# Head of a graph-block kernel: the edge chain moved forward in the written order, its spreading transposes set behind a later product, and one block's one-hot rows moved from ScalarE to VectorE

## The chip, the cores and the metric

The kernel runs on one core of one Trainium2 chip. The metric is the device time of one execution in microseconds (us): the median of three runs, and beside it one profiled execution whose instructions are all recorded. The engines are TensorE (PE, with its weight loads in rows called PEld), VectorE (DVE), ScalarE (ACT), GpSimd (POOL) and SyncE (SP, which here only issues transfers).

## The reference

A graph block on 1250 nodes of 512 features, with 41250 directed edges sorted by destination. Cut to what matters:

```python
xn = layernorm(x)
h  = prelu(xn @ lin_W.T + lin_b, lin_a)
for l in range(2):
    agg = segment_sum(h[src], dst)              # sum over the edges
    h = prelu((h + agg) @ W1[l].T + b1[l], a[l]) @ W2[l].T + b2[l]
    h = relu(batchnorm(h))
x = x + h + linear_attention(xn)                # softmaxed q and k, 8 heads
x = x + merged_experts_ffn(layernorm(x))
```

## The kernel before, in words

The 1250 rows of `x` are ten tiles of up to 128 rows. The kernel turns the edge list into a dense matrix `adj` (source by destination, one added on the diagonal), so that the sum over edges becomes a matrix product. To build `adj`, the sorted edges are cut into 81 blocks of 512. For each block, a window of 24 destinations is found; two sets of one-hot rows are made, `oh_s` (128 wide, by the source's low bits) and `oh_k` (240 wide, by the source's high bits and the destination inside the window); four products on TensorE multiply them, and VectorE adds the 128x240 result to `adj` at the window.

Before any block can be made, the window's start must be known, and this is the **edge chain** of the head, in this order:

- ScalarE copies the destinations to floats (`e_d`, line 746).
- VectorE takes, for each partition, the smallest destination of a block, masks the padding, and takes the largest: three instructions (lines 748, 750 and 751), with the result in `ends`.
- TensorE transposes both halves of `ends` into two PSUM banks `pts` (line 759).
- VectorE reduces each over 128 columns to `span` (line 762).
- TensorE transposes `span` again, broadcast over 128 rows, into `lows` and `highs` (lines 771 and 772; the spreading products).
- VectorE makes `base` (774), its integer copy `base_i` (776) and, in four steps, `key` (784, 785, 788 and 789), and from the sources `s_hi` (766) and `s_lo` (794).

The edges come in by three transfers on SP's queue (lines 661, 663 and 665), which stand behind four tiles of `x` and the four parts of `lw`, and ahead of tiles 4 to 9 of `x`.

The other work of the head is the layer norm of the ten tiles and the first linear layer. Per tile `t`: `x_first(t)` is two VectorE instructions for mean and variance (586, 588) and a square root on ScalarE (590); `x_second(t)` is a reciprocal and a small product on VectorE (595, 596) and the normalising pass on ScalarE (600); `x_third(t)` is four transposes on TensorE and a copy on ScalarE (606, 607). `lin(c0, cn, f)` is eight recorded products on TensorE over `cn` nodes (576), two passes on ScalarE (612, 613, into `h_t` and `u`), and one VectorE instruction that joins them (614).

The order of all this on TensorE, VectorE and ScalarE is written out by hand: the statements stand between `head.enter_context(given(engines={E.PE, E.DVE, E.Activation}))` and `head.close()`, and each of the three engines runs its share in the order of the statements. After `head.close()` a planner, with costs and due times of its own, sets the order at compile time; what is not bound by the written order may also be placed into its gaps. `weave(us)` puts blocks between the products at a pace of 0.70 blocks per planned microsecond; blocks 0 to 2 are made inside the head, the rest behind it. A block's four products are issued once two later blocks have been made (`keep=2`); `oh_s` and `oh_k` have four buffers each.

In every third block ScalarE makes `oh_s` instead of VectorE (`source_rows`: four passes, line 817, and one over all four rows, line 818). The test is `b % 3 == 1 and b > 3`, so block 4 is the first of these, then 7, 10 and so on.

Of the kernel before, what the change touches and what calls it, by code (L numbers as in the profile page):

```python
# [9 lines left out]
F32 = mybir.dt.float32  # L10
# [4 lines left out]
ALU = mybir.AluOpType  # L15
AX = mybir.AxisListType

P = 128
N = 1250
# [12 lines left out]
J = 4  # L32
EB = P * J
NB = (EDGES + EB - 1) // EB
# [10 lines left out]
def rows(t):  # L45
    return min(P, N - t * P)
# [479 lines left out]
def usual_block(  # L526
# [23 lines left out]
    nc = tc.nc  # L550
# [11 lines left out]
    def bank(dtype=F32):  # L562
        return psum.tile([P, 512], dtype, tag="bank", name="bank")
# [10 lines left out]
    def gemm(ps, cn, lhs, rhs, k=DT):  # L574
        for c in range(k):
            nc.tensor.matmul(ps[:, :cn], lhs(c), rhs(c), start=(c == 0), stop=(c == k - 1))  # L576
# [6 lines left out]
    def spread(src, n):  # L583

        st = small.tile([P, 6], F32, name="st")
        nc.vector.bn_stats(st[:n], src)
        mv = small.tile([P, 2], F32, name="mv")
        nc.vector.bn_aggr(mv[:n], st[:n])
        rs = small.tile([P, 2], F32, name="rs")
        nc.scalar.activation(rs[:n, 0:1], mv[:n, 1:2], AF.Sqrt, bias=eps[:n])  # L590
        return mv, rs

    def inverse(mv, rs, n):

        nc.vector.reciprocal(rs[:n, 0:1], rs[:n, 0:1])
        nc.vector.scalar_tensor_tensor(rs[:n, 1:2], mv[:n, 0:1], -1.0, rs[:n, 0:1],
                                       op0=ALU.mult, op1=ALU.mult)

    def normal(dst, src, rs, n):
        nc.scalar.activation(dst, src, AF.Identity, bias=rs[:n, 1:2], scale=rs[:n, 0:1])  # L600

    def to_features(dst, t, src, n):

        pt = bank()
        for c in range(DT):
            nc.tensor.transpose(pt[:, c * P:c * P + n], src[:, c * P:(c + 1) * P], ident[0:n, 0:n])  # L606
        nc.scalar.copy(dst[:, :, t * P:t * P + n], pt.rearrange("p (c n) -> p c n", c=DT)[:, :, 0:n])  # L607

    def prelu(dst, ps, cn, bias, slope):

        u = tmp.tile([P, CHUNKS[0][1]], F32, tag="xt", bufs=4, name="u")
        nc.scalar.activation(dst, ps[:, :cn], AF.Relu, bias=v(*bias))  # L612
        nc.scalar.activation(u[:, :cn], ps[:, :cn], AF.Relu, bias=minus(*bias), scale=-1.0)  # L613
        nc.vector.scalar_tensor_tensor(dst, u[:, :cn], minus(*slope), dst, op0=ALU.mult, op1=ALU.add)  # L614
# [7 lines left out]
    early = count.enter_context(tc.tile_pool(name="early", bufs=1))  # L622
# [22 lines left out]
    edges = early.tile([P, NB, 2, J], I32, name="edges")  # L645
# [50 lines left out]
    def x_first(t):  # L696
        x_live[t] = spread(x_in[0:rows(t), t, :], rows(t))

    def x_second(t):
        n = rows(t)  # L700
        mv, rs = x_live.pop(t)
        inverse(mv, rs, n)
        normal(xn[0:n, t, :], x_in[0:n, t, :], rs, n)

    def x_third(t):
        to_features(xn_t, t, xn[0:rows(t), t, :], rows(t))
# [3 lines left out]
    def lin(c0, cn, f):  # L710
        ps = bank()
        gemm(ps, cn, lambda c: lw[:, c, f * P:(f + 1) * P], lambda c: xn_t[:, c, c0:c0 + cn])
        prelu(h_t[:, f, c0:c0 + cn], ps, cn, ("lin_b", f), ("lin_a", f))
# [22 lines left out]
    x_second(3)  # L736
    lin(0, 256, 0)
    x_third(2)
    x_first(4)
    lin(0, 256, 1)  # L740
    x_third(3)
    x_second(4)
    x_first(5)
    lin(0, 256, 2)
    e_d = early.tile([P, NB, J], F32, name="e_d")
    nc.scalar.copy(e_d, edges[:, :, 1, :])
    ends = early.tile([P, 2, NB], F32, name="ends")
    nc.vector.tensor_reduce(ends[:, 0, :], e_d, AX.X, ALU.min)
    real = early.tile([P, NB, J], F32, name="real")
    nc.vector.scalar_tensor_tensor(real, e_d, float(N), e_d, op0=ALU.is_lt, op1=ALU.mult)  # L750
    nc.vector.tensor_reduce(ends[:, 1, :], real, AX.X, ALU.max)
    x_second(5)
    lin(0, 256, 3)
    x_third(4)
    x_first(6)
    pts = [bank(), bank()]
    lin(256, 256, 0)
    for k in range(2):
        nc.tensor.transpose(pts[k][0:NB, 0:P], ends[:, k, :], ident)
    span = early.tile([NB, 2], F32, name="span")  # L760
    for k, op in ((0, ALU.min), (1, ALU.max)):
        nc.vector.tensor_reduce(span[:, k:k + 1], pts[k][0:NB, 0:P], AX.X, op)
    x_second(6)

    s_hi = early.tile([P, NB, J], I32, name="s_hi")
    nc.vector.tensor_scalar(s_hi, edges[:, :, 0, :], 7, None, op0=ALU.logical_shift_right)
    lin(256, 256, 1)
    x_third(5)
    x_first(7)
    lows, highs = bank(), bank()  # L770
    nc.tensor.transpose(lows[:, 0:NB], span[:, 0:1].to_broadcast([NB, P]), ident[0:NB, 0:NB])
    nc.tensor.transpose(highs[:, 0:NB], span[:, 1:2].to_broadcast([NB, P]), ident[0:NB, 0:NB])
    base = const.tile([P, NB], F32, name="base")
    nc.vector.tensor_scalar(base, lows[:, 0:NB], float(N - W), None, op0=ALU.min)
    base_i = early.tile([1, NB], I32, name="base_i")
# [37 lines left out]
    def source_rows(b, oh_s):  # L813

        off = hot.tile([P, J, P], F16, bufs=2, name="off")
        for j in range(J):
            nc.scalar.activation(off[:, j, :], count16[:, 0:P], AF.Abs, bias=s_lo[:, b, j:j + 1], scale=-1.0)
        nc.scalar.activation(oh_s, off, AF.Relu, bias=1.0, scale=-1.0)  # L818

    def weave(us, keep=2):  # L820

        state["due"] += us * PACE
        while state["block"] < min(NB, state["due"]):
            b = state["block"]
            state["block"] += 1
            oh_s = hot.tile([P, J, P], F16, name="oh_s")
            oh_k = hot.tile([P, J, NT * W], F16, name="oh_k")
            if b % 3 == 1 and b > 3:
                source_rows(b, oh_s)
            for j in range(J):  # L830
                if b % 3 != 1 or b <= 3:
                    nc.vector.tensor_scalar(oh_s[:, j, :], count16[:, 0:P], s_lo[:, b, j:j + 1], None,  # L832
                                            op0=ALU.is_equal)
                nc.vector.tensor_scalar(oh_k[:, j, :], count16, key[:, b, j:j + 1], None, op0=ALU.is_equal)  # L834
            held.append((b, oh_s, oh_k))
            drain(keep)

    def drain(keep):
        while len(held) > keep:
            b, oh_s, oh_k = held.pop(0)  # L840
            if b % 16 == 0:
                k = min(16, NB - b)
                _, state["at"] = nc.values_load_multi_w_load_instructions(
                    base_i[0:1, b:b + k], engines=[mybir.EngineType.DVE], min_val=0, max_val=N - W,
                    skip_runtime_bounds_check_because="both ends are taken from 0 to N - W",
                )
            ps = bank()
            for j in range(J):
                nc.tensor.matmul(ps[:, 0:NT * W], oh_s[:, j, :], oh_k[:, j, :], start=(j == 0), stop=(j == J - 1))  # L849
            at = ds(state["at"][b % 16], W)  # L850
            nc.vector.tensor_tensor(adj_r[:, :, at], adj[:, :, at],  # L851
                                    ps[:, 0:NT * W].rearrange("p (s d) -> p s d", s=NT), ALU.add)
# [3 lines left out]
    for f in range(1, DT):  # L856
        weave(1.4)
        lin(512, 384, f)
        if f < 3:
            x_third(f + 7)  # L860
    head.close()
    for f in range(DT):
        weave(2.4)
        lin(896, 354, f)
# [13 lines left out]
    def k_stage(f):  # L878
        parts = []
        k_m = small.tile([P, 4], F32, name="k_m")  # L880
        for b, (c0, cn) in enumerate(CHUNKS):
            weave(2.8)
            ps = bank()
            gemm(ps, cn, lambda c: wk[:, c, f * P:(f + 1) * P], lambda c: xn_t[:, c, c0:c0 + cn])
            nc.vector.tensor_reduce(k_m[:, b:b + 1], ps[:, :cn], AX.X, ALU.max)
            parts.append(ps)
        nc.vector.tensor_reduce(k_m[:, 3:4], k_m[:, 0:3], AX.X, ALU.max, negate=True)
        k_s = small.tile([P, 4], F32, name="k_s")
        for b, (c0, cn) in enumerate(CHUNKS):
            nc.scalar.activation(k_rows(f)[:, c0:c0 + cn], parts[b][:, :cn], AF.Exp,  # L890
                                 bias=k_m[:, 3:4], accum_out=k_s[:, b:b + 1])

        nc.vector.tensor_reduce(k_s[:, 3:4], k_s[:, 0:3], AX.X, ALU.add)
        nc.vector.tensor_scalar(k_s[:, 3:4], k_s[:, 3:4], float(N) * HD ** 0.5, None, op0=ALU.mult)
        nc.vector.reciprocal(k_z[:, f:f + 1], k_s[:, 3:4])
# [516 lines left out]
def graph_block(tc, *args):  # L1412

    unusual = usual_block(tc, *args)
    with tc.If(unusual > 0):
        general_block(tc, *args)
# [58 lines left out]
```

## Time and profile before

| | us |
|---|---|
| median of three runs | 576.74 (576.42 to 578.34) |
| profiled execution | 576.46 |
| its span, first to last instruction | 574.1 |
| TensorE busy | 546.5 (95%) |
| VectorE busy | 322.7 (56%) |
| ScalarE busy | 241.0 (42%) |
| GpSimd busy | 80.1 (14%) |
| mean granted TensorE clock | 0.981 |

Times inside the execution are counted from the first instruction. An idle stretch ahead of an instruction stands in square brackets with what ended it. TensorE is busy nearly throughout, so only the stretches in which it is not are worth reading closely; the head, the first 60 us, has most of those of the first half.

### The profile page before, as it was taken

The page shows a single profiled execution, that of the slowest core. Times are in us where ns is not written, and L with a number is a line of the kernel's source. Part 1 is how long each engine was busy: PE and PEld are TensorE (multiplying, and loading weights), DVE is VectorE, ACT ScalarE, POOL GpSimd, SP SyncE. Part 2 cuts the span into 40 slices and gives each one's busy share as a digit, 9 for nine tenths or more (in the row PEclk, how much of TensorE's full clock was granted, in tenths as well). Part 3 has the DMA queues.
Part 4 walks back from the last instruction along what each step waited for, and adds up shares of the span by engine and source line. Part 5 has one row for each costly group of instructions (what it writes and reads, how often), then busy time and mean ns, then how long its engine had stood idle before and what let it go on. Part 6 is the DMA issues. An engine that isn't in the chain of part 4 may idle for free.

```text
span 574.1 us, 6955 instructions
## 1 busy us (share of the span) xinstructions
PE 546.5 (95%) x2367; PEld 369.2 (64%) x2367; DVE 322.7 (56%) x1096; ACT 241.0 (42%) x533; POOL 80.1 (14%) x77
## 2 busy tenths in 40 slices
PE   8799999999999999999999999999999989997990
PEld 7665568799955477777854454459995557764540
DVE  4579999977889635444435433111122257707793
ACT  5676654454444112332334433112334355727342
POOL 7200000000000000000013421000000001105975
PEclk9999999999999999999999999999999999997995
DMA  9400200020030020000301002000009020402023
GB/s 287 175 1 1 74 2 1 1 74 2 1 128 20 0 74 0 1 1 1 127 21 55 18 1 73 0 0 1 2 6 365 31 74 1 146 1 75 0 76 110
DMA packets 19285, 29.10 MB, mean 51 GB/s; under 512 B 1529, under 2 KB 8185, under 8 KB 19240
## 3 DMA queue, kind: packets, MB, share of 16 engines
q1 hardware_dynamic: 18984, 28.32, 14.8%
q8 instruction: 20, 0.33, 0.3%
q10 hardware_dynamic: 256, 0.25, 0.2%
q14 instruction: 25, 0.20, 0.1%
HBM read 26.01 MB, written 2.56 MB: 50 GB/s over the span
## 4 chain that ended last, share of the span: by engine, by line
PE 88%; DVE 4%; ACT 3%; POOL 2%; issue 1%; DMA 1%; POOLq 0%; DVEq 0%; ACTq 0%
PE bank L576 28%; PE bank L981 16%; PE bank L968 12%; PE bank L917 6%; PE bank L1034 6%; PE bank L1061 6%; PE bank L849 5%; PE bank L1314 3%; PE bank L606 2%; PE bank L1363 1%; POOL m L1395 1%; POOL m L1396 1%; PE bank L902 1%; DVE bank L1301 1%; PE bank L932 1%
## 5 line engine op out<-in xcount | busy, mean ns | idle before, releaser
L981 PE MATMUL bank<-adj,y_h 128*128 128x416 f32 (+1 forms) x240 | 86.5, 361 | 1.1 <-DVE adj L851 1.1
L981 PE MATMUL bank<-adj,y_l 128*128 128x416 f32 (+1 forms) x240 | 84.4, 352 | 0.0
L834 DVE TENSOR_SCALAR oh_k<-count,e_d 128x240 f16<-128x240 f16 x324 | 82.7, 275 | 0.0
L1080 POOL TENSOR_TENSOR m<-m,ls_bc 128x512 f32<-128x512 f32 (+1 forms) x10 | 12.7, 1268 | 448.8 <-ACT m L600 448.8
L968 PE MATMUL bank<-w,h_t 128*128 128x512 f32 (+1 forms) x160 | 70.4, 592 | 0.0
L576 PE MATMUL bank<-z_t,w 128*128 128x416 f32 (+1 forms) x192 | 68.9, 513 | 0.0
L576 PEld LDWEIGHTS bank<-z_t,w 128*128 128x128 f32 x192 | 36.1, 189 | 31.8 <-issue 30.4
L832 DVE TENSOR_SCALAR oh_s<-count,s_lo 128x128 f16<-128x128 f16 x220 | 54.3, 247 | 0.0
L968 PEld LDWEIGHTS bank<-w,h_t 128*128 128x128 f32 (+1 forms) x160 | 29.4, 188 | 34.8 <-issue 34.5
L614 DVE SCALAR_TENSOR_TENSOR z_t<-u,m_sb,z_t 128x416 f32<-128x416 f32 (+1 forms) x24 | 15.7, 653 | 59.8 <-ACT u L613 59.8
L981 PEld LDWEIGHTS bank<-adj,y_h 128*128 128x128 f32 x240 | 45.1, 188 | 2.6 <-issue 2.1
L981 PEld LDWEIGHTS bank<-adj,y_l 128*128 128x128 f32 x240 | 45.2, 188 | 1.2 <-issue 0.7
L849 PE MATMUL bank<-oh_k,oh_s 128*128 128x240 f16 x324 | 41.3, 266 | 1.3 <-ACT oh_s L818 1.2
L849 PEld LDWEIGHTS <-oh_s 128*128 128x128 f16 x324 | 31.6, 98 | 15.7 <-issue 4.9
L612 ACT ACTIVATE z_t<-bank,v_sb 128x416 f32<-128x416 f32 (+1 forms) x24 | 14.6, 608 | 61.5 <-PE bank L981 61.5
L851 DVE TENSOR_TENSOR adj<-adj,bank 128x240 f32 x81 | 32.3, 399 | 13.9 <-PE bank L849 12.5
L917 PE MATMUL bank<-kk,xn 128*128 128x128 f32 (+1 forms) x320 | 38.4, 275 | 0.0
L995 DVE BATCH_NORM_STATS2 bst<-h_t 128x6 f32<-128x416 f32 (+1 forms) x24 | 14.3, 595 | 42.5 <-ACT h_t L994 42.5
L576 PE MATMUL bank<-xn_t,lw 128*128 128x256 f32 (+2 forms) x128 | 37.6, 439 | 0.3 <-ACT xn_t L607 0.3
L917 PEld LDWEIGHTS bank<-kk,xn 128*128 128x128 f32 (+1 forms) x320 | 37.0, 192 | 0.1
L1061 PE MATMUL bank<-mixer,q_t 128*128 128x512 f32 (+1 forms) x80 | 36.1, 592 | 0.0
L1034 PE MATMUL bank<-wq,xn_t 128*128 128x512 f32 (+1 forms) x80 | 36.0, 592 | 0.0
(165 smaller groups left out, 797.0 us busy)
## 6 DMA issues: line engine op xcount, KB each, us to landing
t<-in_tv_w SPq DMA_DIRECT2D x12, 512.0 KB, 7.4
w<-in_conv_w SPq DMA_DIRECT2D x4, 1024.0 KB, 5.3
x_in<-in_x SPq DMA_DIRECT2D x9, 256.0 KB, 4.7
xt<-in_x SPq DMA_DIRECT2D x9, 256.0 KB, 4.2
out<-m SPq DMA_DIRECT2D x9, 256.0 KB, 2.4
rest<-in_tv_w SPq DMA_DIRECT2D x4, 512.0 KB, 5.1
lw<-in_lin_w SPq DMA_DIRECT2D x4, 256.0 KB, 4.8
wk<-in_w_qkv SPq DMA_DIRECT2D x1, 1024.0 KB, 7.0
```

Source lines behind the costliest of these rows:

```text
L576: nc.tensor.matmul(ps[:, :cn], lhs(c), rhs(c), start=(c == 0), stop=(c == k - 1))
L614: nc.vector.scalar_tensor_tensor(dst, u[:, :cn], minus(*slope), dst, op0=ALU.mult, op1=ALU.add)
L832: nc.vector.tensor_scalar(oh_s[:, j, :], count16[:, 0:P], s_lo[:, b, j:j + 1], None, op0=ALU.is_equal)
L834: nc.vector.tensor_scalar(oh_k[:, j, :], count16, key[:, b, j:j + 1], None, op0=ALU.is_equal)
L849: nc.tensor.matmul(ps[:, 0:NT * W], oh_s[:, j, :], oh_k[:, j, :], start=(j == 0), stop=(j == J - 1))
L851: nc.vector.tensor_tensor(adj_r[:, :, at], adj[:, :, at], ps[:, 0:NT * W].rearrange("p (s d) -> p s d", s=NT), ALU.add)
L917: nc.tensor.matmul(ps[:, c * P:(c + 1) * P], xn[0:n, t, c * P:(c + 1) * P], k_nodes(f)[0:n, t, :], start=(t == 0), stop=(t == NT - 1))
L968: nc.tensor.matmul(ps[:n], h_t[:, c, t * P:t * P + n], w1[:, c, :], start=(c == 0), stop=(c == DT - 1))
L981: nc.tensor.matmul(ps[:, :cn], y[0:n, s, f * P:(f + 1) * P], adj_r[0:n, s, c0:c0 + cn], start=(s == 0 and y is ys[0]), stop=(s == NT - 1 a ...
L1034: nc.tensor.matmul(ps[:n], xn_t[:, c, t * P:t * P + n], wq[:, c, :], start=(c == 0), stop=(c == DT - 1))
L1061: nc.tensor.matmul(ps[:n], q_t[:, h, t * P:t * P + n], mixer[:, h, :], start=(h == 0), stop=(h == DT - 1))
L1314: nc.tensor.matmul(ps[:, :cn], m1[:, c, f * P:(f + 1) * P], xn2_t[:, c, c0:c0 + cn], start=(c == 0), stop=(c == DT - 1))
```

## The change

In the head, six groups of statements change their place in the written order, and one test gets another bound:

- `e_d` on ScalarE moves from behind `lin(0, 256, 2)` to behind `x_third(2)`.
- The three VectorE instructions that make `ends` move from behind `lin(0, 256, 2)` to behind `x_first(4)`, ahead of `lin(0, 256, 1)`.
- The two transposes into `pts` and the two reductions into `span` move from behind `lin(256, 256, 0)` to behind `x_second(5)`, ahead of `lin(0, 256, 3)`.
- `s_hi` moves from behind `x_second(6)` to ahead of it, before `lin(256, 256, 0)`, and `x_second(6)` now stands behind that product.
- `lows` and `highs` stay behind `lin(256, 256, 1)` but move ahead of `x_third(5)` and `x_first(7)`.
- In `weave`, the bound `b > 3` becomes `b > 6` (and `b <= 3` becomes `b <= 6`): block 4's `oh_s` is made by VectorE; ScalarE's first block is 7.

```diff
     x_third(2)
+    e_d = early.tile([P, NB, J], F32, name="e_d")
+    nc.scalar.copy(e_d, edges[:, :, 1, :])
     x_first(4)
+    ends = early.tile([P, 2, NB], F32, name="ends")
+    nc.vector.tensor_reduce(ends[:, 0, :], e_d, AX.X, ALU.min)
+    real = early.tile([P, NB, J], F32, name="real")
+    nc.vector.scalar_tensor_tensor(real, e_d, float(N), e_d, op0=ALU.is_lt, op1=ALU.mult)
+    nc.vector.tensor_reduce(ends[:, 1, :], real, AX.X, ALU.max)
     lin(0, 256, 1)
     x_third(3)
     x_second(4)
     x_first(5)
     lin(0, 256, 2)
-    e_d = early.tile([P, NB, J], F32, name="e_d")
-    nc.scalar.copy(e_d, edges[:, :, 1, :])
-    ends = early.tile([P, 2, NB], F32, name="ends")
-    nc.vector.tensor_reduce(ends[:, 0, :], e_d, AX.X, ALU.min)
-    real = early.tile([P, NB, J], F32, name="real")
-    nc.vector.scalar_tensor_tensor(real, e_d, float(N), e_d, op0=ALU.is_lt, op1=ALU.mult)
-    nc.vector.tensor_reduce(ends[:, 1, :], real, AX.X, ALU.max)
     x_second(5)
-    lin(0, 256, 3)
-    x_third(4)
-    x_first(6)
     pts = [bank(), bank()]
-    lin(256, 256, 0)
     for k in range(2):
         nc.tensor.transpose(pts[k][0:NB, 0:P], ends[:, k, :], ident)
     span = early.tile([NB, 2], F32, name="span")
     for k, op in ((0, ALU.min), (1, ALU.max)):
         nc.vector.tensor_reduce(span[:, k:k + 1], pts[k][0:NB, 0:P], AX.X, op)
-    x_second(6)
+    lin(0, 256, 3)
+    x_third(4)
+    x_first(6)
     s_hi = early.tile([P, NB, J], I32, name="s_hi")
     nc.vector.tensor_scalar(s_hi, edges[:, :, 0, :], 7, None, op0=ALU.logical_shift_right)
+    lin(256, 256, 0)
+    x_second(6)
     lin(256, 256, 1)
-    x_third(5)
-    x_first(7)
     lows, highs = bank(), bank()
     nc.tensor.transpose(lows[:, 0:NB], span[:, 0:1].to_broadcast([NB, P]), ident[0:NB, 0:NB])
     nc.tensor.transpose(highs[:, 0:NB], span[:, 1:2].to_broadcast([NB, P]), ident[0:NB, 0:NB])
+    x_third(5)
+    x_first(7)
...
-            if b % 3 == 1 and b > 3:
+            if b % 3 == 1 and b > 6:
                 source_rows(b, oh_s)
             for j in range(J):
-                if b % 3 != 1 or b <= 3:
+                if b % 3 != 1 or b <= 6:
```

## Prediction

> **What bounds the kernel now.** I read the page first, then the waits of the first 60 us, then each engine's timeline there, and last the granted clock by the microsecond. The page says that only TensorE's gaps are worth anything:
>
> ```profile
> PE 546.5 (95%) x2367; PEld 369.2 (64%) x2367; DVE 322.7 (56%) x1096; ACT 241.0 (42%) x533; POOL 80.1 (14%) x77
> ```
>
> TensorE's timeline shows three gaps of the edge chain and its blocks (start, duration, then the idle time before it):
>
> ```profile
> 19.60 0.31 PE L759 MATMUL bank<-ident,ends 128*81 128x128 f32 x1 [0.63 <-DVE rs L595]
> ...
> 24.52 0.28 PE L771 MATMUL bank<-ident,span 81*128 81x81 f32 x1 [2.44 <-DVE span L762]
> ...
> 47.65 0.28 PE L849 MATMUL bank<-oh_k,oh_s 128*128 128x240 f16 x1 [1.20 <-ACT oh_s L818]
> ```
>
> Together 4.27 us, and the change aims at all three. But TensorE's waits are not the head's chain. The chain of waits runs, up to 24 us, back and forth between VectorE and ScalarE. VectorE's timeline shows what the edge chain puts into it:
>
> ```profile
> 14.77 0.48 DVE L614 SCALAR_TENSOR_TENSOR h_t<-u,m_sb,h_t 128x256 f32<-128x256 f32 x1 [1.15 <-ACT u L613]
> ...
> 18.05 0.48 DVE L748 TENSOR_REDUCE ends<-e_d 128x81 f32<-128x324 f32 x1
> 18.45 0.48 DVE L750 SCALAR_TENSOR_TENSOR real<-e_d 128x324 f32<-128x324 f32 x1
> 18.96 0.49 DVE L751 TENSOR_REDUCE ends<-real 128x81 f32<-128x324 f32 x1
> 19.37 0.15 DVE L595 RECIPROCAL rs<-rs 128x1 f32<-128x1 f32 x1
> ...
> 24.18 0.48 DVE L762 TENSOR_REDUCE span<-bank 81x1 f32<-81x128 f32 x2
> 24.58 0.15 DVE L595 RECIPROCAL rs<-rs 128x1 f32<-128x1 f32 x1
> ```
>
> The reciprocals of tiles 5 and 6 stand behind the edge chain, and ScalarE waits for them:
>
> ```profile
> 13.71 0.29 ACT L590 ACTIVATE rs<-mv,eps 128x1 f32<-128x1 f32 x1 [0.96 <-DVE mv L588]
> ...
> 17.35 0.46 ACT L746 CAST e_d<-edges 128x324 f32<-128x324 int32 x1
> 19.75 0.81 ACT L600 ACTIVATE xn<-x_in,rs 128x512 f32<-128x512 f32 x1 [1.95 <-DVE rs L596]
> ```
>
> From 37 us VectorE makes one-hot rows, and up to 76 us it is as tight as TensorE:
>
> ```profile
> 51.70 0.59 DVE L614 SCALAR_TENSOR_TENSOR h_t<-u,m_sb,h_t 128x354 f32<-128x354 f32 x1 [0.24 <-ACT u L613]
> ...
> 54.50 0.59 DVE L614 SCALAR_TENSOR_TENSOR h_t<-u,m_sb,h_t 128x354 f32<-128x354 f32 x1 [0.62 <-ACT u L613]
> ...
> 74.85 0.66 DVE L834 TENSOR_SCALAR oh_k<-count,e_d 128x240 f16<-128x240 f16 x3
> 75.02 0.98 PE L849 MATMUL bank<-oh_k,oh_s 128*128 128x240 f16 x8
> ```
>
> Block 19's rows end at 75.51 and TensorE takes the last at 75.74: a slack of 0.23 us (0.05 at block 2, 0.20 at block 11). Afterwards it grows: block 32's rows end at 98.44, and TensorE takes them at 103.14. So a gain reaches the end only if VectorE too comes to block 19 earlier; behind that TensorE alone sets the pace.
>
> **The change, part by part.** One engine's instruction is costed by the distance to its successor's start.
>
> (a) `e_d` on ScalarE: 0.36 us, now behind tile 2's copy, which starts at 12.17 and frees the engine at about 12.66. There lies the 0.96 us wait shown at 13.71: cost nothing. If that cover failed, 0.36 us would fall on the chain. The edges must have landed. The second of their three transfers lands at 10.77, and packets under 512 bytes, which only these edges have in numbers there, fill 9.25 to 10.0. The third transfer's landing is not shown; tile 5 of x, issued behind it, lands at 12.16. A rule speaks against leaning on that: "DMA: Bandwidth & Descriptors", Queues, rings and completion order, says that transfers of one issuing engine do not complete in order. By the rows I take 11.5 and no wait; by the rule the landing is open, and each 1 us beyond 13.1 would hold the square root of tile 4 and all of ScalarE behind it by 1 us. I go by the packets.
>
> (b) The three instructions of `ends`, 18.05 to 19.37, are 1.32 us on VectorE's path. At the new place they start behind tile 4's variance, at 13.67, in the 1.15 us wait shown at 14.77, and free the engine at 14.96: 0.15 to 0.19 too late. Net -1.15 us for tile 5's reciprocal and what follows.
>
> (c) The two reductions to `span` (24.18 to 24.58, 0.40 us) now stand behind tile 5's reciprocal, about 18.55 to 18.95, where VectorE next waits for `u` of `lin(0, 256, 3)` (1.60 us at 21.32 before). Net -0.40 us for tile 6 on. `s_hi` (0.40 us) moves from one wait into another: nothing; without that wait it costs its 0.40.
>
> (d) TensorE: the transposes into `pts` take 0.24 us and wait about 0.2 for `ends`, so `lin(0, 256, 3)` starts 0.46 later, at 15.2. It ends near 17.1, and ScalarE takes it at 19.3: covered. The spreading products come behind `lin(256, 256, 1)` at 20.9, and `span` is ready at 19.0: the waits of 0.63 and 2.44 us go. `lin(256, 256, 2)` starts 3.3 us earlier. But what is late next is ScalarE, only 1.55 us earlier: tile 6's transposes need its normalised rows (24.3, a wait of 1.0), `lin(512, 384, 0)` needs tile 6's copy (27.9, a wait of 1.5), tile 9 costs another 0.6. Of 3.3 us, about 1.75 are given back; the first block and `s_lo` come 1.55 us earlier. PSUM: by this lay-out at most seven of the eight banks are held at once (lows and highs until 29), so no bank wait is added. No transfer is moved in any queue; SP and POOL issue what they did, in the same order.
>
> (e) Block 4: VectorE gets four instructions of 0.163, +0.65 us; ScalarE loses four passes of 0.29 and one of 0.66. TensorE's 1.20 us wait becomes a wait for VectorE, whose first pair of block 4 now comes at 46.33 + 0.36 + 0.1 (hand-over) = 46.8 instead of ScalarE's 47.60, and whose last pair comes 0.65 later: I keep 0.6 of the 1.20. `lin(896, 354, 1)` and `(…, 2)` then end earlier, and VectorE's idle 0.24 and 0.62 us, which waited for their `u`, close: -0.86. An idle 0.42 us at 43.65, behind five ScalarE passes of which some belonged to block 4, should close by about half: -0.2; how the planner refills ScalarE there is not shown, so 0 to -0.42.
>
> (f) The clock. Before, the clock granted fell after the 2.44 us gap:
>
> ```profile
> 26.00:27.00 1.00, 1.00 (x4) 0.75 (x3) 0.47 (x2) 0.97 (x3) 0.00 (x0) 0.59 0.00 0
> ...
> 29.00:30.00 1.00, 1.00 (x5) 0.82 (x4) 0.96 (x4) 0.66 (x2) 0.00 (x0) 0.70 0.00 0
> ```
>
> (the last number but two is the clock). Half speed for 3.3 us costs TensorE 1.6 us, yet VectorE set block 2's time, so little of it reached the end. Afterwards the gaps are 1.0 and 1.5 us. "TensorE: Matmul & The Clock Gate", HAM oscillation, warns of idle gaps over about 3.4 us: by that rule the dip before should not have come and none comes after. The row shows that 2.44 was enough, so gaps of 2.5 in total within 5 us may do it too. One such dip costs TensorE 1.6 us; laid over the gaps of (d) it delays the first block's products by 0.1 to 0.9, all before VectorE's limit at block 2. By rule or row my sum is the same; I count 0.
>
> The sum at block 19: -1.55 + 0.65 - 0.86 - 0.2 = -1.96 us. Behind it the rest moves as a whole. The profiled execution took 576.46 (0.28 under the median): 576.46 - 1.96 = 574.5 us.
>
> **The rivals.**
> 1. A part only: the waits stay in other places (a dip that outlasts the slack by 1 us, block 4 still late, nothing closed at 51.70 and 54.50). Without the 0.86 and the 0.2: -0.9, so 575.6. For it: the planner sets the order from 44 us on anew, and slack at blocks 2, 11, 15 and 19 is under 0.25.
> 2. All gaps pass through: -4.27, so 572.2. For it: TensorE is 95% busy and heads the chain from 25 us. Against: tile 6's rows and copy above.
> 3. Slower, by the clock: the gaps that replace one long one are spread over 23 to 38 us and keep the clock at half for four stretches of 3.4 us, 13.6 us in all. TensorE loses 6.8 us. It has the waits of 1.5, 0.6 and 0.2 in the head to absorb 2.3 of it, the 0.6 won at block 4, and the lead of 1.55: +2.35 us, so 578.8. It decides once the dip is longer than about 9 us, twice the sum of these covers. For it: a dip of 6.9 us stands at 521.1 in this trace, after several short gaps. Against: the dip of the head before ended after 3.3 us.
> 4. The edges are not there at 12.66: each late microsecond is lost; +1 us lands at 575.4.
>
> **How the numbers follow.** The forecast has 0.52; rival 1 (with 4) 0.24; rival 2 0.10; rival 3 0.14. A measurement of this kernel tells about 0.3% (1.7 us) from no change. The forecast's own range, 573.6 to 575.2 from the bounds in (e) and 0.4 of hand-over, lies mostly past that line (0.42 of 0.52); rival 2 is faster; rival 1 is within it; of rival 3, 0.12 is slower. So faster 0.52, same 0.36, slower 0.12. The range leaves out rival 2's and rival 3's far ends: 572.6 to 577.2.
>
> **What would show it.** No wait at lines 759 above 0.3 us and none at 771; tile 5's normalising pass near 18.6 instead of 19.75; `s_lo` near 35.1 instead of 36.69; new TensorE waits for ScalarE (lines 606 and 576) of about 2.5 us in total between 23 and 29; block 4's wait near 0.6 and from VectorE; block 19 taken near 73.6. Wrong would be: `s_lo` 3 us earlier (rival 2), a clock of 0.5 for over 9 us before 45 (rival 3), `e_d` waiting for a transfer (rival 4), or a block beyond 19 that makes TensorE wait.

## The result, and the profile after

The changed kernel takes 575.92 us (median of ten runs, 574.24 to 576.37) against 576.98 of the kernel before; the ratio is 0.9971, with a 95% interval of 0.9958 to 0.9985. The forecast was 574.5 us for a profiled execution of 576.46, a ratio of 0.9966. The measured 0.29% lies on the 0.3% line between "faster" and "the same", where the forecast had leaned to "faster".

The profiled execution of the changed kernel shows none of this at first sight: it took 576.37 us with a span of 574.4, against 574.1 before. The gain must be looked for by stage. TensorE's timeline in the head, with the transposes of `ends` at line 755 now and the first spreading product at 769:

```profile
14.91 0.57 PE L755 MATMUL bank<-ident,ends 128*81 128x128 f32 x2
...
20.95 0.23 PE L769 MATMUL bank<-ident,span 81*128 81x81 f32 x1
...
24.25 0.66 PE L606 MATMUL bank<-ident,xn 128*128 128x128 f32 x4 [0.83 <-ACT xn L600]
...
27.85 2.85 PE L576 MATMUL bank<-xn_t,lw 128*128 128x384 f32 x8 [1.22 <-ACT xn_t L607]
...
45.28 0.26 PE L849 MATMUL bank<-oh_k,oh_s 128*128 128x240 f16 x1 [0.38 <-DVE oh_k L834]
```

The waits of 0.63 and 2.44 us at the edge chain are gone. In their place TensorE waits 0.83 us for tile 6's normalised rows and 1.22 us for its copy (`lin(512, 384, 0)` at line 576 needs it); block 4's wait has fallen from 1.20 to 0.38 and is for VectorE. VectorE's timeline:

```profile
13.65 0.46 DVE L743 TENSOR_REDUCE ends<-e_d 128x81 f32<-128x324 f32 x1
...
18.19 0.15 DVE L595 RECIPROCAL rs<-rs 128x1 f32<-128x1 f32 x1
18.37 0.16 DVE L596 SCALAR_TENSOR_TENSOR rs<-mv,rs 128x1 f32<-128x1 f32 x1
18.45 0.48 DVE L758 TENSOR_REDUCE span<-bank 81x1 f32<-81x128 f32 x2
...
35.14 0.49 DVE L794 SCALAR_TENSOR_TENSOR s_lo<-s_hi,edges 128x324 f32<-128x324 int32 x1
...
42.52 0.62 DVE L614 SCALAR_TENSOR_TENSOR h_t<-u,m_sb,h_t 128x384 f32<-128x384 f32 x1 [0.42 <-ACT u L613]
```

Tile 5's reciprocal starts at 18.19 instead of 19.37, and `s_lo` at 35.14 instead of 36.69. ScalarE's timeline answers to it:

```profile
12.75 0.48 ACT L740 CAST e_d<-edges 128x324 f32<-128x324 int32 x1
13.82 0.29 ACT L590 ACTIVATE rs<-mv,eps 128x1 f32<-128x1 f32 x1 [0.60 <-DVE mv L588]
...
18.57 0.81 ACT L600 ACTIVATE xn<-x_in,rs 128x512 f32<-128x512 f32 x1 [0.94 <-DVE rs L596]
```

`e_d` fills part of the old 0.96 us wait and itself waits for nothing. The 0.24 and 0.62 us waits of VectorE near 52 and 54 us have no counterpart: from 48 to 56 us its timeline shows no wait at all. Block 19's last product is taken at 73.72 (75.74 before), and block 80's first at 199.74 (201.75 before): 2.01 us ahead, and the stretch between is carried over as a whole. These are the two products on TensorE, after and then before:

```profile
73.72 0.26 PE L849 MATMUL bank<-oh_k,oh_s 128*128 128x240 f16 x1
...
199.74 0.57 PE L849 MATMUL bank<-oh_k,oh_s 128*128 128x240 f16 x4
```

```profile
75.74 0.27 PE L849 MATMUL bank<-oh_k,oh_s 128*128 128x240 f16 x1
...
201.75 0.57 PE L849 MATMUL bank<-oh_k,oh_s 128*128 128x240 f16 x4
```

The 2.01 us are lost late in this one execution. In both kernels TensorE has a gap of 1.89 us near 466 us, where it waits for ScalarE's last pass of a batch norm (line 1008). Again after and then before:

```profile
466.01 1.07 PE L1151 MATMUL bank<-ident,h_t 128*128 128x128 f32 x5 [1.89 <-ACT h_t L1008]
466.91 5.29 PE L1061 MATMUL bank<-mixer,q_t 128*128 128x512 f32 x8
```

```profile
468.05 1.06 PE L1151 MATMUL bank<-ident,h_t 128*128 128x128 f32 x5 [1.89 <-ACT h_t L1008]
468.95 3.60 PE L1061 MATMUL bank<-mixer,q_t 128*128 128x512 f32 x8
```

By the microsecond (the last number but two is the granted clock), the changed kernel's profiled execution:

```profile
467.00:468.00 1.00, 1.00 (x3) 0.34 (x2) 0.93 (x4) 0.21 (x1) 0.00 (x0) 0.72 0.00 0
...
469.00:470.00 1.00, 1.00 (x3) 0.48 (x2) 0.96 (x3) 0.99 (x2) 0.00 (x0) 0.50 0.00 0
470.00:471.00 1.00, 1.00 (x3) 0.43 (x2) 0.96 (x4) 0.00 (x0) 0.00 (x0) 0.57 0.00 0
```

The eight products behind the gap take 5.29 us there, and 3.60 in the profiled execution of before, whose clock stays at 1.00 at this place. That is 1.69 us given back. A last 0.6 goes near 528 us, at the end of a fall of the clock of 6.83 us that both executions have, at 521.1 us before and at 522.1 after. The execution of before has its other fall at 26 to 30 us instead, in the head. So both show a mean clock of 0.981, and the two spans agree by accident.

### The profile page after: what moved, and what is told of

Its sections match the earlier page's. It is cut to its first block, busy times and chain, and to the rows that moved or that the text cites. A ratio compares the mean times of both kernels' runs of the same rounds, so it can differ in the third digit from the quotient of the medians.

```text
span 574.4 us, 6950 instructions
## 1 busy us (share of the span) xinstructions
PE 548.2 (95%) x2367; PEld 368.4 (64%) x2367; DVE 323.0 (56%) x1100; ACT 240.0 (42%) x528; POOL 80.2 (14%) x77
## 4 chain that ended last, share of the span: by engine, by line
PE 86%; DVE 3%; ACT 3%; DMA 3%; POOL 2%; SPq 1%; issue 1%; POOLq 0%; DVEq 0%; ACTq 0%
PE bank L576 25%; PE bank L981 16%; PE bank L968 12%; PE bank L1061 6%; PE bank L917 6%; PE bank L1034 6%; PE bank L849 6%; PE bank L1314 3%; DMA g2bc<-in_g2b_col 2%; PE bank L606 1%; PE bank L1363 1%; POOL m L1395 1%; DMA edges<-in_e_full 1%; POOL m L1396 1%; PE bank L902 1%
## 5 line engine op out<-in xcount | busy, mean ns | idle before, releaser
L849 PE MATMUL bank<-oh_k,oh_s 128*128 128x240 f16 x324 | 43.0, 266 | 0.6 <-DVE oh_k L834 0.4
L1061 PE MATMUL bank<-mixer,q_t 128*128 128x512 f32 (+1 forms) x80 | 37.8, 615 | 0.0
L576 PE MATMUL bank<-xn_t,wk 128*128 128x416 f32 (+1 forms) x96 | 36.2, 514 | 0.0
```

What stands on the lines that cost most here:

```text
L1061: nc.tensor.matmul(ps[:n], q_t[:, h, t * P:t * P + n], mixer[:, h, :], start=(h == 0), stop=(h == DT - 1))
```

## The experiments

Two theories stood against each other after the forecast. The first: the alternation of VectorE and ScalarE sets the head's pace, and the gain is what leaves that chain, carried on because VectorE sets the pace up to block 19. The second: TensorE's waits are the gain. Executions start with some tenths of scatter (tile 2's normalising pass starts between 9.20 and 9.73), so in this table block 80's first product is counted from that pass, and set against the 192.55 us of before.

Four recorded executions with the changed kernel's head agree in this count within 0.07 us. Two with the head of before do not: in the one whose gap at 466 us is filled it is 192.86, because there the half clock of the head came 1.0 us earlier, ScalarE waited 0.17 us for `lin(256, 256, 2)`, and `s_lo` and all behind it came 0.30 later. So a difference of up to 0.3 us from before says nothing, and the changed kernel's gain is 2.1 to 2.4 us.

| kernel | tile 2's pass | `s_lo` | wait at the spreading products | wait at block 4 | block 80's first product | counted from the pass, against before |
|---|---|---|---|---|---|---|
| before | 9.20 | 36.69 | 2.44 | 1.20 | 201.75 | 0 |
| changed | 9.31 | 35.14 | 0 | 0.38 | 199.74 | -2.12 |
| head alone | 9.21 | 34.98 | 0 | 1.20 | 200.04 | -1.72 |
| block 4 alone | 9.30 | 36.80 | 2.44 | 0.38 | 201.39 | -0.46 |
| spreading products later | 9.50 | 37.22 | 0.80 | 1.20 | 202.28 | +0.23 |
| `ends` alone | 9.73 | 35.94 | 1.85 | 1.20 | 201.01 | -1.27 |
| another order on top (`s_lo` itself moved forward) | 9.39 | 25.79 | 0 | 0 | 197.28 | -4.66 |

Counted from the pass, block 80 moves with `s_lo` in every one of these kernels but the last: `s_lo` comes 1.67 us earlier in the changed kernel, 1.72 with the head alone, 1.28 with `ends` alone, and 0.22 later with the spreading products later. Block 80 follows each to 0.01 us, and where block 4's rows are on VectorE another 0.46 is added. So what counts is when VectorE can start the rows.

**The head alone.** The changed kernel with the old bound of `source_rows`:

```diff
-            if b % 3 == 1 and b > 6:
+            if b % 3 == 1 and b > 3:
-                if b % 3 != 1 or b <= 6:
+                if b % 3 != 1 or b <= 3:
```

> The changed kernel with block 4's one-hot rows left on ScalarE. By the forecast (the head's gain is what the VectorE-ScalarE chain wins, 1.55 us, and block 4's move adds 0.4): s_lo at 35.1 to 35.2 as in the changed kernel; TensorE waits about 1.2 us at block 4 for ScalarE; block 80's first product at about 200.2 (201.75 before, 199.74 changed); time 1.5 us under before. By the rival that block 4's move is the whole gain: block 80 at 201.7 and no gain.

Median 575.35 (22 runs) against 577.19 before; ratio 0.9971 (0.9962 to 0.9981). The head carries 1.72 of the 2.12 us, and block 4's wait for ScalarE is 1.20 as before:

```profile
45.94 0.28 PE L849 MATMUL bank<-oh_k,oh_s 128*128 128x240 f16 x1 [1.20 <-ACT oh_s L818]
```

**Block 4 alone.** The kernel before with the new bound:

```diff
-            if b % 3 == 1 and b > 3:
+            if b % 3 == 1 and b > 6:
-                if b % 3 != 1 or b <= 3:
+                if b % 3 != 1 or b <= 6:
```

> The kernel before with block 4's rows on VectorE and nothing else changed. By the forecast: s_lo stays at 36.7, TensorE's wait at block 4 falls from 1.20 to about 0.5, VectorE's 0.24 and 0.62 us waits near 52 and 54 close and pay for the added 0.65, so block 80's first product comes at about 201.35 (0.4 earlier than before). By the rival that block 4's move is the gain: 199.7, 2 us earlier.

Median 577.05, ratio 0.9994 (0.9984 to 1.0004). The 0.46 us at block 80 are there, where 0.4 was expected; the time itself cannot tell them from nothing. By itself this is little more than the 0.3 by which before differs from itself; but with the head moved too the new bound is worth 0.40 (2.12 less 1.72), between heads that scatter by 0.07. The two parts add up: 1.72 and 0.46 against 2.12 together. The rival that block 4 is the gain falls.

**The spreading products later, and nothing else.** The kernel before with `lows`, `highs`, `base` and `base_i` moved behind `lin(256, 256, 2)`:

```diff
     lin(256, 256, 1)
     x_third(5)
     x_first(7)
-    lows, highs = bank(), bank()
...
     lin(256, 256, 2)
+    lows, highs = bank(), bank()
...
     x_third(6)
```

> The kernel before with only the two spreading products, and base and base_i behind them, moved behind lin(256, 256, 2): it takes TensorE's 2.44 us wait away without freeing VectorE or ScalarE of anything. By the forecast: the wait at the spreading products is gone, the same time comes back as waits for tile 6's rows and copy, s_lo stays within 0.2 of 36.69, block 80's first product within 0.3 of 201.75, time unchanged. By the rival that TensorE's waits are the gain: block 80 at about 199.4 and 2.4 us saved.

Median 577.09, ratio 1.0006 (0.9997 to 1.0015). TensorE's timeline of this kernel shows what became of the 2.44 us:

```profile
24.76 0.26 PE L772 MATMUL bank<-ident,span 81*128 81x81 f32 x1 [0.80 <-DVE span L762]
...
25.97 0.66 PE L606 MATMUL bank<-ident,xn 128*128 128x128 f32 x4 [0.76 <-ACT xn L600]
...
29.57 2.85 PE L576 MATMUL bank<-xn_t,lw 128*128 128x384 f32 x8 [1.21 <-ACT xn_t L607]
```

0.80 us of waiting is left at the spreading products (it had been expected to vanish), and 1.97 us come back as waits for tile 6. `s_lo` and block 80 come 0.5 us later than before, outside the 0.2 and 0.3 that were expected, but 0.3 of it is the later start of this execution: counted from the pass it is 0.22 and 0.23. So 1.64 us of waiting taken from TensorE, without freeing the other two engines, is worth nothing here, where the second theory wanted 2.4. This decides between the two theories.

**`ends` alone.** The kernel before with only `e_d` and the three instructions of `ends` at their new places:

```diff
     x_third(2)
+    e_d = early.tile([P, NB, J], F32, name="e_d")
...
     x_first(4)
+    ends = early.tile([P, 2, NB], F32, name="ends")
...
     lin(0, 256, 2)
-    e_d = early.tile([P, NB, J], F32, name="e_d")
...
     x_second(5)
```

> The kernel before with only e_d and the three instructions of ends moved forward to where the changed kernel has them; the transposes, the reductions to span and the spreading products stay, and so does block 4 on ScalarE. By the forecast's terms: VectorE's chain wins 1.15 us (s_lo at 35.5 instead of 36.69), while TensorE still waits 2 to 2.5 us at the spreading products; block 80's first product 1.15 earlier, at 200.6; time 1.1 us under before. By the rival that TensorE's wait is what counts: its wait stays, so no gain.

Median 576.96 against 577.22, ratio 0.9983 (0.9972 to 0.9994). TensorE still waits at the spreading products, and block 80 comes 1.27 us earlier:

```profile
23.76 0.28 PE L771 MATMUL bank<-ident,span 81*128 81x81 f32 x1 [1.85 <-DVE span L762]
```

That is term (b), forecast at 1.15. By itself this run does not tell the theories apart: the wait at the spreading products fell by 0.59 and the one of 0.63 at line 759 is gone, so TensorE too waits 1.22 less. The medians differ by only 0.26, where 1.1 was expected: half of these runs have the mean clock of 0.978, and about a third of before's. Between runs of one mean clock it is 1.05 (577.25 against 578.30 at 0.978) and 0.80 (575.44 against 576.24 at 0.984).

**The gap at 466 us filled.** The changed kernel, and the kernel before, each with 16 transposes that nobody reads:

```diff
     last_order.enter_context(given())
+    dead = bank()
+    for i in range(16):
+        nc.tensor.transpose(dead[:, 0:P], ident, ident)
```

> The changed kernel with 16 transposes of the identity that nobody reads, put into TensorE's 1.89 us gap at 464 to 466 us. Theory: the changed kernel gains 2.0 us up to block 80, and in most runs pays 1.7 of them back where the clock falls to 0.5 from 467.3 to 470.7. Then with the gap filled the clock stays 1.00 there in every run, the mean granted clock is 0.984 throughout, and the median falls by 1.5 to about 574.4. If the dip is not due to that gap: 0.981 and about 576 as without the filling, or 0.1 to 0.3 us more for the dead products.

> The kernel before with the same 16 unread transposes in the same gap, here at 466 to 468 us. If the clock's fall behind that gap comes in some of its runs (those near 578.3) and not in others (near 576.4), then with the gap filled the slower group is gone and the median comes to about 576.6; the changed kernel with the same filling (574.7) then stands 1.9 to 2.0 us under it, which is the gain of the head alone. If the two groups of times have another cause, they stay.

Changed and filled: 574.70 us (573.74 to 574.85, five runs). Before and filled: 576.51 (575.88 to 577.61), which is 0.9985 (0.9976 to 0.9995) of before unfilled. The filled pair differs by 1.81 us, expected 1.9 to 2.0; the two were measured in different sets, whose unfilled kernel before stood at 577.19 and 577.22. In the filled changed kernel no run is left near 576, where eight of the unfilled kernel's first ten were, and neither filled profile shows a fall of the clock at that place. One filled run still has a mean clock of 0.981, so the mean alone doesn't say where the clock fell. Of the filled kernel before no run lies above 577.61, where the unfilled one has 17 of 43 above 578; but a group of four runs remains at 577.25 to 577.61, with a mean clock of 0.978 or 0.979, and no trace shows where their clock fell.

**Once more, and later.** Does the change itself bring that fall of the clock, by making the gap come 2 us earlier? The changed kernel was run again, and once with 19 unread transposes ahead of the second layer's first product:

```diff
+    dead = bank()
+    for i in range(19):
+        nc.tensor.transpose(dead[:, 0:P], h_t[:, DT - 1, 0:P], ident)
     ys = y_stage(1, h_t, w1, ("C", "D"), lambda t: None)
```

> The changed kernel once more, for the share of its runs that pay for the clock's fall behind the gap at 466 us (mean clock 0.981 against 0.984): 8 of its first 10 runs did, and about a third to a half of the runs of before. If the change itself brings the fall (because that gap now comes 2 us earlier), about 8 in 10 again and a median near 576.0. If the share is one half whatever the kernel: a median near 575.3 and 3 us under the slow group of before.

> The changed kernel with 19 unread transposes of h_t (2.07 us) ahead of the second layer's first product, so that everything from there on, the gap at 466 included, comes at the same time as in the kernel before. If the fall of the clock hangs on that time, its share drops to that of before and the median is 2.07 - 0.8 above the changed kernel's, near 577.0. If it does not, the share stays and the median is 2.07 above the changed kernel's in the same call, near 578 or 577.4.

The second set of the changed kernel: 574.29 us against 577.02, ratio 0.9948 (0.9928 to 0.9967), with one of six runs near 576 instead of eight of ten. Its profiled execution has the same head (block 80 at 199.71) and a span of 572.1, because the clock stays:

```profile
467.00:468.00 1.00, 1.00 (x4) 0.46 (x3) 0.93 (x4) 0.18 (x1) 0.00 (x0) 1.00 0.00 0
...
469.00:470.00 1.00, 1.00 (x4) 0.49 (x3) 0.97 (x3) 0.96 (x2) 0.00 (x0) 1.00 0.00 0
```

Of all 16 runs of the changed kernel, nine have the lower clock (median 575.9) and seven the higher (574.2). The delayed kernel took 577.35 us, 3.06 above the changed kernel beside it, with 12 of 22 runs at the lower clock. Its median falls between the two expectations and decides nothing; 9 in 16 and 12 in 22 are about the same share, so there is no sign that the fall hangs on the gap's time. With eight of ten in one set and one of six in the next, shares of so few runs can't say more. The unread products cost 2.5 us within the group of the higher clock (576.74 against 574.24) instead of 2.07. In the trace all that stands behind them comes 2.35 us later, and the gap ends at 468.35.

**Which executions pay.** The twelve traces say more than the shares. In each, the granted clock changes only on a grid: every stretch at one clock that begins and ends inside the execution is a multiple of 3.41 us, and the grid lies differently against the program each time. In the changed kernel's first profile, 0.72 in the row of 467 and 0.57 in that of 470 put the fall at 467.4 to 470.9, and the grid interval ahead of it, 464.0 to 467.4, holds the whole gap (464.1 to 466.0). In its second profile a grid line at 464.7 cuts the gap in two, and the clock stays. Up to 500 us there are seven falls in all twelve, each behind an interval with 1.74 to 2.45 us of idle TensorE; the most idle time that no fall follows is 1.83. If the grid lies at random, the gap of 1.89 us lies within one interval in (3.41 - 1.89) / 3.41 = 45% of executions, an estimate from these numbers and near 9 in 16. No run moved the grid on purpose, and near 520 us idle time alone does not tell: falls come there behind as little as 0.5 us of it.

**Another order on top.** If the alternation of VectorE and ScalarE is the pace, more can be had from it. The changed kernel with these moves:

```diff
-    x_second(5)
     pts = [bank(), bank()]
...
     x_third(4)
+    x_second(5)
     x_first(6)
...
-    x_second(6)
     lin(256, 256, 1)
+    x_second(6)
...
+    s_lo = early.tile([P, NB, J], F32, name="s_lo")
+    nc.vector.scalar_tensor_tensor(s_lo, s_hi, -float(P), edges[:, :, 0, :], op0=ALU.mult, op1=ALU.add)
+    x_first(8)
     key = e_d
...
     x_first(9)
+    nc.vector.tensor_tensor(key, key, real, ALU.add)
+    nc.vector.scalar_tensor_tensor(key, s_hi, float(W), key, op0=ALU.mult, op1=ALU.add)
     lin(512, 384, 0)
```

> The changed kernel with a few more statements of the head in another order: x_second(5) behind x_third(4), x_second(6) behind lin(256, 256, 1), x_first(8) and s_lo ahead of key, the last two steps of key behind x_first(9). If the alternation of VectorE and ScalarE sets the head's pace (ScalarE waits for a tile's reciprocal while a finished product stands ready for it), then s_lo and key are ready 4 us earlier, block 0's first product comes 2.8 earlier than in the changed kernel (34.4 instead of 37.22), and block 80's 2.5 to 3.5 earlier (196.7); time about 573.0 with a clock of 0.981. If TensorE or the rest of VectorE's queue sets the pace instead, at most 1 us.

> The same order with the gap at about 462 us filled as well. Theory: the clock stays at 1.00 there, so the time is the filled changed kernel's 574.7 less 2.5 to 3.5, near 571.7: under both kernels. If the later order does not help: 574.7.

571.61 us (571.46 to 571.83, four runs): 0.9896 (0.9875 to 0.9917) of before, and under both kernels. ScalarE's timeline shows one part of the mechanism:

```profile
17.60 0.47 ACT L612 ACTIVATE h_t<-bank,v_sb 128x256 f32<-128x256 f32 x1
...
19.41 0.81 ACT L600 ACTIVATE xn<-x_in,rs 128x512 f32<-128x512 f32 x1 [0.50 <-DVE rs L596]
```

`lin(0, 256, 3)`'s passes start at 17.60, as soon as the product is done, instead of standing at 19.29 behind tile 5's normalising pass, which waits for VectorE. Tile 5 itself comes 0.84 later (19.41 against 18.57), but the products no longer wait for it. VectorE joins `lin(512, 384, 0)` at 33.15 instead of 34.60, 1.45 us earlier, and `s_lo`, 0.40 us, no longer stands between this and the rows, which start at 33.96 instead of 35.81. `key` was expected 4 us earlier and is not: its last step starts at 32.20, against 31.72 in the changed kernel. How the gain divides among the moves was not tested. Block 0's first product comes at 35.33 (34.4 expected) instead of 37.22, block 80's at 197.28: 2.5 us earlier than in the changed kernel, at the lower end of what was expected. (The 573.0 us expected for the time had the lower clock in it; these four runs have the higher.) With the gap filled too, the time is 571.69 us (571.10 to 572.29, four runs): no better, since by their mean clock (0.983 and 0.984) none of the four unfilled runs paid for the gap; its range is wider, and the two cannot be told apart.

## Why the prediction was right, point by point

- **(a) `e_d`** costs nothing: it starts at 12.75 and waits for no transfer, so the edges had landed, and rival 4 falls. The rule that transfers of one issuing engine need not complete in order ("DMA: Bandwidth & Descriptors" in the Trainium skill, section "Queues, rings and completion order") leaves the landing open and is not contradicted; going by the packets was right here.
- **(b) and (c)**: forecast 1.15 and 0.40. `ends` alone gives 1.27 at block 80. The whole head brings `s_lo` 1.71 us earlier in the kernel with the head alone (34.98 against 36.69, at the same start), so about 0.4 is left for `span`.
- **(d)**: the 2.44 and 0.63 us are gone and came back as waits for tile 6, as laid out. They measure 0.83 and 1.22 instead of 1.0 and 1.5; tile 9, laid out at 0.6, shows 0.09. The sum of (d) did not come out even as written: 1.0, 1.5 and 0.6 are 3.1 and not 1.75, and block 0's first product comes 2.25 us earlier (37.22 instead of 39.47), not 1.55. It did no harm, since `s_lo`, 1.55 earlier, is what counts. Rival 2, that all gaps pass through, falls with the spreading products moved alone.
- **(e)**: the forecast let 0.6 us of block 4's wait of 1.20 remain, though its own 46.8 against 47.60 leaves 0.4; 0.38 remain, and the two waits of VectorE closed. The third, 0.42 us at 43.65, did not close: it stands at 42.52 in the profile after. There the planner has put five passes of line 817 ahead of `lin(512, 384, 3)`'s again, now of later blocks. That -0.2 was wrong. What made up for it was not forecast: VectorE's last rows of block 19 used to be ready 0.23 us before TensorE took them, and now are 0.05 us before.
- **(f)**: after gaps of 0.83 and 1.22 us the clock stayed at 1.00 in the head, and rival 3, a long fall there, did not come. Both the page's rule and the row of the clock before allowed these gaps one by one; the guess that 2.5 us of gaps within 5 us may do it too was not put to the test, since they came to 2.05. The warning of idle gaps over about 3.4 us ("TensorE: Matmul & The Clock Gate" in the Trainium skill, section "HAM oscillation") gives no safe bound in this case: falls followed single gaps of 2.44 us before and of 1.89 us at 466 us after. And the fall in the head of before was counted at 0, but it cost 0.30 us in the second recorded execution.
- **The sum at block 19** was -1.96; TensorE takes block 19's last product 2.02 us earlier, and block 80's 2.01. So close a match is partly luck: the -0.2 that failed and the 0.18 of slack that was used up cancel, and before differs from itself by 0.3. The first set's 575.92 lies nearer to rival 1's 575.6, but not by rival 1's way: block 4 is no longer late, the waits at 51.70 and 54.50 closed, and block 80 came the whole 2.0 us earlier.
- **"The rest moves as a whole"** is the step that was too simple. It holds up to 464 us. Behind it stands a gap of 1.89 us that the forecast gave no term: in 9 of 16 runs, by their mean clock, the clock falls behind it, which costs 1.7 us each time. Before has such runs too (the profile of block 4 alone shows both falls, in the head and behind the gap, with a mean clock of 0.978), so the difference of the medians is near the head's gain only over many runs: 1.1 us in the first set, 2.7 in the second, 1.81 with the gap filled. The mean came out because both kernels pay; a term of plus or minus 1.7 us for a single median belonged into the working. The full range, 572.6 to 577.2, holds both groups of the changed kernel (574.2 and 575.9), though it was drawn for other reasons; the forecast's own 573.6 to 575.2 misses the first set's 575.92.

## What to carry to other kernels

In a head where three engines run in a written order, the wait to remove is the one on the chain: here 1.64 us of TensorE's wait of 2.44, taken away by themselves, were worth nothing, and 1.3 us of VectorE's instructions, moved into a stretch in which VectorE waited anyway, were worth nearly all they cost. Look next for an engine that holds finished work behind an instruction that still waits for another engine: an order that puts the waiting one behind, and that also moved `s_lo`, brought another 2.5 us here. Compare by the arrival of a fixed instruction some way behind the edit before comparing totals, since a late fall of the clock can hide the gain in any one execution; and record the kernel before more than once, as it differed from itself by 0.3 us here.

## What was not expected of the hardware

- A TensorE gap of 1.89 us is followed by about 3.4 us at half the clock in some executions of one kernel and not in others: 9 of 16 runs here, by their mean clock. In the traces up to 500 us the fall comes where nearly the whole gap lies within one interval of a 3.41 us grid. Gaps of 0.83 and 1.22 us in the head of the changed kernel were not followed by one.
- Filling such a gap with products that nobody reads is worth 0.15% (0.05 to 0.24%) in the kernel before.
